# Silu as one ScalarE function instead of tanh and a multiply, in a two-layer sequence kernel

## The chip, the cores and the metric

The kernel runs on one core of a Trainium2 chip. The core has a matmul engine (TensorE, PE in the profile; its weight loads are shown apart as PEld), VectorE (DVE), ScalarE (ACT, the engine of the activation functions), GpSimd (POOL) and SyncE (SP, which here only issues DMAs). The engines run side by side, each through its own list of instructions in order, and wait for one another through semaphores. TensorE writes to PSUM, a small memory of banks; the other operands lie in SBUF. The metric is the device time of one execution in microseconds.

## The reference: what is computed

Two layers work on x of 2 x 1024 tokens with 512 features, each as an attention-like part and a feed-forward part; after every part the result is added to x and normalized over the features. Cut to what matters here:

```python
# layer 0, attention part: silu on q, k and v
q = silu(x @ Wq); k = silu(x @ Wk); v = silu(x @ Wv)      # 16 heads of 32
o = lightning_attn(q, k, v, log_decay)                     # chunks of 128 tokens
o = rmsnorm_per_head(o * sigmoid((x @ Wg1) @ Wg2)) * w
x = layernorm(x + o @ Wo)
# layer 0, feed-forward: silu on the gate, then a Walsh-Hadamard transform
x = layernorm(x + fwht(silu(x @ W1.T) * (x @ W3.T)) @ W2.T)
# layer 1, selective scan: for each of 512 features and 32 states
delta = softplus(dt + b_dt)
h = exp(delta * A) * h + delta * u * B                     # step by step in time
y = sum_over_states(h * C) + u * D
x = layernorm(x + y)
# layer 1, feed-forward: silu on the gate
x = layernorm(x + (silu(x @ Wg) * (x @ Wu)) @ Wdown)
```

All of it is float32.

## The kernel before

**Tiling and phases.** The tokens are cut into five groups (`GROUPS`, line 38): three of four chunks of 128 tokens and two of two chunks, at the beginning and the end of one sequence. A group passes through four phases, listed in `PHASES` (line 40): V computes the values, A is the rest of the attention, F the feed-forward part of layer 0, f that of layer 1. The scan of a group (class `Scan`) runs beside these phases: it begins after the group's F and must be finished before its f. The Hadamard transform is folded into W2 once at the start, on VectorE (`butterflies`) and TensorE (`w2_products`).

**The order of the work.** A planner (`Order`, line 61) builds the program. Every part of the kernel is a generator (a thread) that yields `Op`s: an engine, an estimated duration, the buffers read and written, and a priority. The planner keeps a clock for every engine, finds for each engine the op that can start, takes among ops that are ready the one of the lowest `prio`, and writes the instructions in the order of its own estimated times. So an estimate that is changed reorders the whole program. Estimates of ScalarE's work come from `act` (line 254): 0.26 us and 0.82 ns per column.

**Tables.** ScalarE holds the tables of one set of functions at a time; a function of another set is preceded by an instruction that loads its tables (ACT_TABLE_LOAD in the profile). The planner keeps one name for what is loaded (`self.table`): an op with another `table` gets 1.3 us more, and among ready ops of equal priority one that needs no load goes first (`wrong`, line 161). Before the change there are two names, "tanh" and "log". The set that has tanh has exp too, and so does the set of the logarithm (`natural_log_exp_and_others`, which `log_tables`, line 448, loads). So the exponentials of the scan carry no name: they run with either.

**Silu before.** The product x @ W lies in a PSUM bank. `silu2` (line 531, for q, k and v) has ScalarE write tanh(x/2) to a buffer `th` (through `tanh_half`, line 455), and VectorE then forms (tanh(x/2) + 1) * x, which is twice silu (line 536). In the feed-forward phases `hidden` (line 1014) does the same into the tile h (lines 455 and 1025), and VectorE multiplies by the second product (line 1030). The surplus factors of two are taken out elsewhere: the decays of the attention are scaled by 0.125, the transformed W2 by 0.5, and the last feed-forward phase scales its sum by 0.5 when it is added (line 1072). The attention's sigmoid gate also uses tanh (line 731).

**The scan.** A unit is one state of two blocks of 128 features over a four-chunk group (or of four blocks over a two-chunk group). For a unit GpSimd forms delta * u * B into `dbu` (line 1332, five buffers); ScalarE writes exp(delta * A) into `da`, a pair of PSUM banks with two buffers (line 1352); VectorE runs the recurrence over `da` and `dbu` (line 1379) and multiplies by C (line 1392); GpSimd sums up the results (lines 1422, 1428 and a DMA that accumulates, issued at line 264). If the sequence goes on in a later group, ScalarE copies the last state (line 1404). The `da` buffer comes free when both have read it. The scan's VectorE ops have a priority below that of the attention and feed-forward ops.

**Around silu on TensorE.** All matmul results other than `da` share four PSUM banks ("mm"). `product` (line 986) makes the gate's and the second product of the feed-forward phase (matmul line 994), `sums_of` (line 1049) the product with W2 or the down matrix (line 1053). In the attention `project` makes q and k (line 615), `values` makes v (line 565); k is transposed (line 682) and scaled (line 689), scores are made (line 793) and scaled (line 811), outputs are collected (lines 837 and 845), gated, normalized (lines 864 to 896) and mixed (line 940).

Of the kernel before, what the change touches and what calls it, by code (L numbers as in the profile page):

```python
# [11 lines left out]
ALU = mybir.AluOpType  # L12
# [4 lines left out]
P = 128  # L17
# [43 lines left out]
class Order:  # L61
# [25 lines left out]
    def begin(self, op):  # L87
# [53 lines left out]
    def run(self):  # L141
        while True:
# [6 lines left out]
            for th in list(self.threads):  # L149
# [30 lines left out]
def two_layers(  # L180
# [73 lines left out]
    def act(cols, fn, **kw):  # L254
        return Op("ACT", 0.26 + cols * 0.82e-3, fn, **kw)

# [104 lines left out]
    dmh_b = [Buf() for _ in range(EB)]  # L361
    ident_b, consts_b, decays_b, scan_b, early_b, mask_b, hadamard_b = (Buf() for _ in range(7))

# [10 lines left out]
    def load_consts():  # L374
# [45 lines left out]
        yield Op("ACT", 2.0, decays, r=[consts_b, early_b], w=[raw])  # L420
# [21 lines left out]

        yield Op("ACT", 0.8, state_decays, r=[raw], w=[scan_b])

    class Tables:
        log = False

    def log_tables():

        if not Tables.log:  # L450
            nc.scalar.preload_act_table_set("natural_log_exp_and_others")
        Tables.log = True

    def tanh_half(dst, src):
        nc.scalar.activation(dst, src, AF.Tanh, scale=0.5)  # L455
        Tables.log = False

# [39 lines left out]
    def normalized(gi, c, stage, store=None):  # L497
# [14 lines left out]
        def scales():  # L512
# [8 lines left out]
            "ACT", 1.6, scales, r=[s],  # L521
            w=[xb] if store is not None else [xb, there[gi, c, stage]], table="log", prio=-2,
        )
# [6 lines left out]

    def silu2(dst, bank):

        th = Buf()
        yield act(512, lambda: tanh_half(th.t, bank.t), r=[bank], a=[("th", th)], table="tanh")
        yield dve(
            512, lambda: nc.vector.scalar_tensor_tensor(  # L536
                dst.t, th.t, 1.0, bank.t, ALU.add, ALU.mult
            ),
            r=[bank, th], a=[("h", dst)], free=[bank, th],
        )  # L540
# [12 lines left out]
    def front(gi):  # L553
# [6 lines left out]
        def values(c):  # L560
            bank = Buf()

            def mm():
                for k in range(EB):
                    nc.tensor.matmul(  # L565
                        bank.t, xT.t[:, k, c * P : (c + 1) * P], w_v[k].t,
                        start=k == 0, stop=k == EB - 1,
                    )

            yield pe(  # L570
                mm_us(EB, 512), mm, r=xT.reads(c, c + 1) + w_v, a=[("mm", bank)],
                free=w_v if c == n - 1 else [],
            )
            spawn(silu2(v2[c], bank))

# [6 lines left out]
    def attention(gi, nxt, prio):  # L582
# [26 lines left out]
        def project(j, vb):  # L609
# [14 lines left out]
            )  # L624
            spawn(silu2((qT, kT)[j][vb], bank))

# [20 lines left out]
        def head_decays():  # L647

            for eb in range(EB):
# [15 lines left out]
                if gi == 0:  # L665
                    yield Op("ACT", 1.5, made, r=[early_b, consts_b], a=[("dm", b)])
                    b.written = None
                    yield dve(512, masked, r=[mask_b], w=[b])
                    yield dma(KB256, lambda: dmh[eb], lambda: b.t, r=[b], w=[dmh_b[eb]],
# [4 lines left out]
        def block(vb):  # L674
# [41 lines left out]
            def gate(bank=Buf()):  # L716
# [12 lines left out]
                def tanh():  # L729
                    yield act(  # L730
                        512, lambda: tanh_half(sg.t, bank.t), r=[bank], a=[("sg", sg)],
                        free=[bank], table="tanh",
                    )
# [144 lines left out]
            def norm():  # L878
# [12 lines left out]

                yield Op("ACT", 1.3, rstd, r=[bank], w=[sg], free=[bank], table="log")

# [78 lines left out]

    def ffn(ph, gi, xT, whole, down_scale, store, after=None):

# [4 lines left out]
        for fh in range(halves):  # L979
# [34 lines left out]
            def hidden(f):  # L1014

                t, pg, pu = hT[f], pss[f, 0], pss[f, 1]
                yield act(
                    512, lambda: tanh_half(t.t, pg.t), r=[pg], a=[("h", t)], table="tanh"
                )
                t.written = None  # L1020
                if fh == halves - 1 and f == 7:
                    reached(ph)

                def gated():
                    nc.vector.scalar_tensor_tensor(t.t, t.t, 1.0, pg.t, ALU.add, ALU.mult)  # L1025
# [103 lines left out]
    def w2_products(dq, f, b):  # L1129

        cols = slice(dq * q_d, (dq + 1) * q_d)
        for c4 in range(4):
# [29 lines left out]
    class Scan:  # L1162
# [74 lines left out]
        def softplus(self, k, bank, u):  # L1237
# [11 lines left out]
            def logs():  # L1249
# [9 lines left out]
            yield Op(  # L1259
                "ACT", 4 * (0.25 + T * 0.82e-3), logs, w=[r], a=[("th", a)], table="log",  # L1260
                prio=late,
# [81 lines left out]
        def decays(self):  # L1343
# [157 lines left out]
    def phase(i):  # L1501
# [8 lines left out]
        elif ph[0] == "F":  # L1510
            spawn(scan_inputs(gi), -0.5)
            yield from ffn(ph, gi, results[gi], False, 1.0, None)
        else:
            xT = Columns(gi)
            for c in range(chunks(gi)):
                yield from turn(xT, gi, c, 3)
            yield from ffn(ph, gi, xT, False, 0.5, row_of(gi))

# [81 lines left out]
```

## Time and profile before

| | |
|---|---|
| median of three runs | 1909.76 us (1906.78 to 1911.31) |
| time of the profiled execution | 1910.39 us |
| its span in the trace | 1908.6 us |
| TensorE busy | 1807.7 us, 95% of the span |
| VectorE busy | 1432.8 us, 75% |
| ScalarE busy | 868.4 us, 45% |
| GpSimd busy | 1069.5 us, 56% |
| table loads on ScalarE | 94, of 1283 ns each |

The profile is of one execution. Its page gives busy time by engine, the span in 40 equal slices (each digit the busy share in tenths; PEclk is the clock granted to TensorE, in tenths of full speed), the chain of work that ended last, and groups of instructions by line. The trace behind it can be asked for waits (who waited for whom, total, times, longest), for stretches of time (busy time of each engine in each) and for single instructions in order of time. The tanh of q, k and v appears as `th<-mm`, that of the feed-forward gate as `h<-mm`, and that of the attention's own gate as `sg<-mm`, all at line 455.

### The profile page before, as it was taken

The numbers are of one execution on the slowest core, as the hardware profiler recorded it, in microseconds if no ns is written. First come the engines' busy times: TensorE is split into PE (matmuls) and PEld (weight loads), VectorE is DVE, ScalarE is ACT, GpSimd is POOL, SyncE is SP. The second block draws the span as 40 slices with busy tenths as digits, with TensorE's granted clock in tenths as the row PEclk, the third lists the DMA queues.
The fourth block names the chain that finished last, engine by engine and source line by source line (L and its number), as shares of the span: only waits on it lengthen the run. The fifth ranks groups of instructions, "written<-read, shape, count | busy, mean of one in ns | idle before, by whom it ended". The sixth has DMA issues, their size and how long they took to land.

```text
span 1908.6 us, 19111 instructions
## 1 busy us (share of the span) xinstructions
PE 1807.7 (95%) x6160; PEld 988.7 (52%) x6160; DVE 1432.8 (75%) x1747; ACT 868.4 (45%) x1605; POOL 1069.5 (56%) x558
## 2 busy tenths in 40 slices
PE   6989988999999799998799999999799999999998
PEld 3666544445755454444554454444586444544575
DVE  6521389992217999999899999999989999998221
ACT  2420565442244553458553457555434635743221
POOL 0000156760024778898568988867778886776000
PEclk8999998999999899998799999999899999999999
DMA  8635335662555366776446867767589684665252
GB/s 246 177 120 168 121 105 130 163 165 60 162 165 206 100 175 165 213 187 178 120 122 166 218 145 204 201 204 225 161 231 253 169 210 152 188 177 149 72 160 72
DMA packets 212084, 315.22 MB, mean 165 GB/s; under 512 B 19984, under 2 KB 121744, under 8 KB 211984
## 3 DMA queue, kind: packets, MB, share of 16 engines
q1 hardware_dynamic: 193408, 250.56, 41.9%
q0 software_dynamic: 16272, 59.25, 16.8%
q10 hardware_dynamic: 2304, 4.20, 0.6%
q8 instruction: 49, 0.80, 0.2%
q14 instruction: 51, 0.42, 0.1%
HBM read 236.34 MB, written 18.35 MB: 133 GB/s over the span
## 4 chain that ended last, share of the span: by engine, by line
PE 79%; DVE 12%; ACT 3%; DMA 3%; issue 2%; SPq 1%; POOL 0%; DVEq 0%; ACTq 0%
PE mm L994 43%; PE mm L1053 22%; DVE da L1379 5%; PE mm L615 4%; DVE dbu L1392 2%; PE mm L565 2%; PE mm L940 2%; DVE sc L811 1%; PE mm L793 1%; PE mm L479 1%; SPq L264 1%; PE mm L845 1%; DMA C<-rows 1%; PE mm L837 1%; PE mm L745 1%
## 5 line engine op out<-in xcount | busy, mean ns | idle before, releaser
L994 PE MATMUL mm<-xT,w 128*128 128x256 f32 (+1 forms) x2704 | 898.9, 493 | 9.0 <-DVE h L1025 6.4
L994 PEld LDWEIGHTS mm<-xT,w 128*128 128x128 f32 x2704 | 516.8, 192 | 386.3 <-issue 323.2
L1332 POOL TENSOR_TENSOR dbu<-du,B 128x1024 f32<-128x1024 f32 x256 | 630.7, 2479 | 128.4 <-DMA y<-dbu 111.4
L1352 ACT ACTIVATE da<-delta,a_s 128x512 f32<-128x512 f32 (+1 forms) x640 | 386.4, 605 | 260.9 <-DVE dbu L1392 238.9
L1053 PE MATMUL mm<-w,h 128*128 128x512 f32 x1024 | 449.0, 594 | 2.1 <-DVE xn L1076 2.1
L1379 DVE TENSOR_TENSOR_SCAN da<-da,hlast,dbu 128x512 f32<-128x512 f32 (+1 forms) x384 | 425.4, 1108 | 10.6 <-ACT da L1352 5.3
L1428 POOL TENSOR_TENSOR y<-y,dbu 128x1024 f32<-128x1024 f32 x123 | 306.2, 2490 | 98.9 <-DVE dbu L1392 96.9
L1392 DVE TENSOR_TENSOR dbu<-da,C 128x1024 f32<-128x1024 f32 x256 | 312.3, 1220 | 6.0 <-ACT hlast L1404 0.7
L1053 PEld LDWEIGHTS mm<-w,h 128*128 128x128 f32 x1024 | 194.0, 191 | 234.7 <-issue 226.2
L1379 DVE TENSOR_TENSOR_SCAN da<-da,dbu 128x256 f32<-128x256 f32 (+1 forms) x256 | 245.6, 959 | 6.1 <-ACT da L1352 2.5
L1234 POOL TENSOR_TENSOR xn<-xn,dp 128x512 f32<-128x512 f32 x16 | 23.1, 1452 | 312.6 <-PE mm L479 312.6
L1025 DVE SCALAR_TENSOR_TENSOR h<-h,mm 128x512 f32<-128x512 f32 x128 | 87.1, 680 | 129.0 <-ACT h L455 128.8
L455 ACT ACTIVATE h<-mm 128x512 f32<-128x512 f32 x128 | 76.1, 595 | 220.6 <-PE mm L994 220.0
L1030 DVE TENSOR_TENSOR h<-h,mm 128x512 f32<-128x512 f32 x128 | 87.2, 682 | 84.0 <-PE mm L994 83.4
L1404 ACT COPY hlast<-da 128x2 f32<-128x2 f32 (+1 forms) x160 | 25.4, 159 | 228.1 <-DVE dbu L1392 182.4
L615 PE MATMUL mm<-xT,w 128*128 128x512 f32 (+1 forms) x320 | 118.0, 518 | 3.3 <-DVE sc L811 1.8
L264 POOL DMA_DIRECT2D y<-dbu x113 | 102.5, 907 | 20.3 <-DVE dbu L1392 16.5
L615 PEld LDWEIGHTS mm<-xT,w 128*128 128x128 f32 x320 | 60.2, 193 | 53.5 <-issue 44.1
L514 ACT ACTIVATE rstd<-mv,eps 128x1 f32<-128x1 f32 x64 | 18.6, 290 | 135.9 <-DVE mv L509 135.8
L940 PE MATMUL mm<-w,xT 128*128 128x512 f32 x128 | 66.8, 669 | 12.7 <-DVE xT L896 11.0
L536 DVE SCALAR_TENSOR_TENSOR h<-th,mm 128x512 f32<-128x512 f32 x48 | 32.5, 682 | 45.2 <-ACT th L455 45.0
L565 PE MATMUL mm<-w,xT 128*128 128x512 f32 x128 | 60.7, 623 | 3.1 <-DMA w<-in_wv_dram 2.8
(91 smaller groups left out, 1246.3 us busy)
## 6 DMA issues: line engine op xcount, KB each, us to landing
y<-dbu POOLq DMA_DIRECT2D x113, 512.0 KB, 6.2
w<-in_wgut_dram SPq DMA_DIRECT2D x160, 256.0 KB, 4.1
B<-rows SPq DMA_DIRECT2D x128, 256.0 KB, 4.2
C<-rows SPq DMA_DIRECT2D x128, 256.0 KB, 3.7
w<-in_w1t_dram SPq DMA_DIRECT2D x80, 256.0 KB, 4.4
w<-in_w3t_dram SPq DMA_DIRECT2D x80, 256.0 KB, 4.3
w<-w2h SPq DMA_DIRECT2D x80, 256.0 KB, 4.1
w<-in_wdnt_dram SPq DMA_DIRECT2D x80, 256.0 KB, 2.9
```

Of the source, the lines that this page charges most:

```text
L264: return Op(eng, us, lambda: of.dma_start(dst(), src(), **more), dma=nbytes, **kw)
L565: nc.tensor.matmul(bank.t, xT.t[:, k, c * P : (c + 1) * P], w_v[k].t, start=k == 0, stop=k == EB - 1,)
L615: nc.tensor.matmul(bank.t[:, s * T : (s + 1) * T], w_qk[j][k].t[:, eb * P : (eb + 1) * P], xT.t[:, k, :], start=k == 0, stop=k == EB - 1,)
L940: nc.tensor.matmul(accs[c].t, oT.t[:, k_, c * P : (c + 1) * P], w_o[k_].t, start=k_ == 0, stop=k_ == EB - 1,)
L994: nc.tensor.matmul(bank.t[:, s * T + c0 * P : s * T + c1 * P], blocks[fb // 2][j][k // 2].t[:, k % 2 * 2 * P + k0 : k % 2 * 2 * P + k0 + P ...
L1030: 512, lambda: nc.vector.tensor_mul(t.t, t.t, pu.t), r=[pu], w=[t], free=[pu]
L1053: nc.tensor.matmul(accs[c].t, hT[f // S].t[:, s * T + c * P : s * T + (c + 1) * P], w_d[f].t, start=f == 0, stop=f == 8 * S - 1,)
L1332: 1024, lambda: nc.gpsimd.tensor_mul(self.wide(self.db[i]), self.wide(du), self.row(self.bs, i)),
L1352: nc.scalar.activation(d[:, j, :], self.wide(delta)[:, j, :], AF.Exp, scale=a_s[:, k0 + j, n : n + 1],)
L1379: nc.vector.tensor_tensor_scan(d()[:, j, :], d()[:, j, :], self.wide(db)[:, j, :], init, ALU.mult, ALU.add,)
L1392: 1024, lambda: nc.vector.tensor_mul(self.wide(db), d(), self.row(self.cs, i)),
L1428: 1024, lambda: nc.gpsimd.tensor_add(y.t, y.t, db[i].t), r=o, w=[y],
```

## The change

Silu becomes one ScalarE instruction, from PSUM straight to the tile where it is needed. The VectorE steps at lines 536 and 1025 go, and with them the buffer `th` for q, k and v, and the scalings that took out the factors of two. The attention's sigmoid gate keeps its tanh. The function silu lies in a set of tables that has tanh but not exp. So every op now names the sets that it can run with, the exponentials of the scan too; the planner counts a switch when the loaded set is none of them, and then takes the first one named as loaded. The estimate of a ScalarE op also changes.

```diff
+EXP, LOG, TANH, SILU = ("exp", "log"), ("log",), ("exp", "silu"), ("silu",)
...
+    def switches(self, op):
+        return op.table is not None and self.table not in op.table
...
-        if op.table is not None and op.table != self.table:
+        if self.switches(op):
             us += 1.3
-            self.table = op.table
+            self.table = op.table[0]
...
-                wrong = op.table is not None and op.table != self.table
+                wrong = self.switches(op)
...
     def act(cols, fn, **kw):
-        return Op("ACT", 0.26 + cols * 0.82e-3, fn, **kw)
+        return Op("ACT", 0.18 + cols * 0.81e-3, fn, **kw)
...
-        yield dve(
-            P, lambda: nc.vector.tensor_scalar_mul(early[:, 2, :], early[:, 2, :], 0.125),
-            r=[early_b], w=[mask_b],
-        )
...
-        yield dve(512, lambda: nc.vector.tensor_scalar_mul(q_dec, q_dec, 0.125), r=[raw],
-                  w=[decays_b])
...
     def log_tables():
-        if not Tables.log:
+        if order.table != "log":
             nc.scalar.preload_act_table_set("natural_log_exp_and_others")
-        Tables.log = True
-
-    def tanh_half(dst, src):
-        nc.scalar.activation(dst, src, AF.Tanh, scale=0.5)
-        Tables.log = False
+
+    def silu(dst, src):
+        nc.scalar.activation(dst, src, AF.Silu)
...
-    def silu2(dst, bank):
-        th = Buf()
-        yield act(512, lambda: tanh_half(th.t, bank.t), r=[bank], a=[("th", th)], table="tanh")
-        yield dve(
-            512, lambda: nc.vector.scalar_tensor_tensor(
-                dst.t, th.t, 1.0, bank.t, ALU.add, ALU.mult
-            ),
-            r=[bank, th], a=[("h", dst)], free=[bank, th],
+    def to_silu(dst, bank):
+        yield act(
+            512, lambda: silu(dst.t, bank.t), r=[bank], a=[("h", dst)], free=[bank], table=SILU
         )
...
                 yield act(
-                    512, lambda: tanh_half(t.t, pg.t), r=[pg], a=[("h", t)], table="tanh"
+                    512, lambda: silu(t.t, pg.t), r=[pg], a=[("h", t)], free=[pg], table=SILU
                 )
...
-                def gated():
-                    nc.vector.scalar_tensor_tensor(t.t, t.t, 1.0, pg.t, ALU.add, ALU.mult)
-
-                yield dve(512, gated, r=[pg], w=[t], free=[pg])
-                t.written = None
...
-                    if down_scale != 1.0:
-                        nc.vector.scalar_tensor_tensor(
-                            xb.t, bank.t, down_scale, xb.t, ALU.mult, ALU.add
-                        )
-                    else:
-                        nc.vector.tensor_add(xb.t, bank.t, xb.t)
+                    nc.vector.tensor_add(xb.t, bank.t, xb.t)
...
-                    b.t[:, s4, :].rearrange("p c d -> p (c d)"), bank.t, 0.5 / math.sqrt(FF)
+                    b.t[:, s4, :].rearrange("p c d -> p (c d)"), bank.t, 1.0 / math.sqrt(FF)
...
                         self.T, exp, r=[delta, scan_b] + ([da] if j else []),
                         a=[] if j else [("da", da)],
                         free=[delta] if i + len(self.delta) >= U and j == self.W - 1 else [],
+                        table=EXP,
```

The softplus, the normalizations and the attention's rsqrt carry `table=LOG` in place of `"log"`, the attention gate's tanh `table=TANH`, and the decays that are made once at the start `table=EXP`.

More of the change, by code (lines that the diff above doesn't have):

```diff
@@ L361, in two_layers @@
     dmh_b = [Buf() for _ in range(EB)]
-    ident_b, consts_b, decays_b, scan_b, early_b, mask_b, hadamard_b = (Buf() for _ in range(7))
+    ident_b, consts_b, decays_b, scan_b, early_b, hadamard_b = (Buf() for _ in range(6))
     def load_first():
@@ L412, in decays @@
                 )
-        yield dve(
-            P, lambda: nc.vector.tensor_scalar_mul(early[:, 2, :], early[:, 2, :], 0.125),
-            r=[early_b], w=[mask_b],
-        )
         raw = Buf()
-        yield Op("ACT", 2.0, decays, r=[consts_b, early_b], w=[raw])
-        yield dve(512, lambda: nc.vector.tensor_scalar_mul(q_dec, q_dec, 0.125), r=[raw],
-                  w=[decays_b])
+        yield Op("ACT", 2.0, decays, r=[consts_b, early_b], w=[decays_b], table=EXP)
         yield dma(
@@ L441, in state_decays @@
             nc.scalar.mul(a_s, a_s, -1.0)
-        yield Op("ACT", 0.8, state_decays, r=[raw], w=[scan_b])
-    class Tables:
-        log = False
+        yield Op("ACT", 0.8, state_decays, r=[raw], w=[scan_b], table=EXP)
     def log_tables():
-        if not Tables.log:
+        if order.table != "log":
             nc.scalar.preload_act_table_set("natural_log_exp_and_others")
-        Tables.log = True
-    def tanh_half(dst, src):
-        nc.scalar.activation(dst, src, AF.Tanh, scale=0.5)
-        Tables.log = False
+    def silu(dst, src):
+        nc.scalar.activation(dst, src, AF.Silu)
     class Columns:
@@ L521, in normalized @@
             "ACT", 1.6, scales, r=[s],
-            w=[xb] if store is not None else [xb, there[gi, c, stage]], table="log", prio=-2,
+            w=[xb] if store is not None else [xb, there[gi, c, stage]], table=LOG, prio=-2,
         )
@@ L573, in values @@
             )
-            spawn(silu2(v2[c], bank))
+            spawn(to_silu(v2[c], bank))
         for c in range(n):
@@ L624, in project @@
             )
-            spawn(silu2((qT, kT)[j][vb], bank))
+            spawn(to_silu((qT, kT)[j][vb], bank))
         def gates():
@@ L665, in head_decays @@
                 if gi == 0:
-                    yield Op("ACT", 1.5, made, r=[early_b, consts_b], a=[("dm", b)])
+                    yield Op("ACT", 1.5, made, r=[early_b, consts_b], a=[("dm", b)],
+                             table=EXP)
                     b.written = None
-                    yield dve(512, masked, r=[mask_b], w=[b])
+                    yield dve(512, masked, r=[early_b], w=[b])
                     yield dma(KB256, lambda: dmh[eb], lambda: b.t, r=[b], w=[dmh_b[eb]],
@@ L730, in tanh @@
                     yield act(
-                        512, lambda: tanh_half(sg.t, bank.t), r=[bank], a=[("sg", sg)],
-                        free=[bank], table="tanh",
+                        512, lambda: nc.scalar.activation(sg.t, bank.t, AF.Tanh, scale=0.5),
+                        r=[bank], a=[("sg", sg)], free=[bank], table=TANH,
                     )
@@ L890, in rstd @@
                     nc.scalar.activation(sg.t, sg.t, AF.Exp, scale=-0.5)
-                yield Op("ACT", 1.3, rstd, r=[bank], w=[sg], free=[bank], table="log")
+                yield Op("ACT", 1.3, rstd, r=[bank], w=[sg], free=[bank], table=LOG)
                 def scaled():
@@ L970, in attention, with ffn @@
             yield from turn(nxt, gi, c, 1)
-    def ffn(ph, gi, xT, whole, down_scale, store, after=None):
+    def ffn(ph, gi, xT, whole, store, after=None):
         n, T = chunks(gi), tokens(gi)
@@ L1259, in softplus @@
             yield Op(
-                "ACT", 4 * (0.25 + T * 0.82e-3), logs, w=[r], a=[("th", a)], table="log",
+                "ACT", 4 * (0.25 + T * 0.82e-3), logs, w=[r], a=[("th", a)], table=LOG,
                 prio=late,
@@ L1511, in phase @@
             spawn(scan_inputs(gi), -0.5)
-            yield from ffn(ph, gi, results[gi], False, 1.0, None)
+            yield from ffn(ph, gi, results[gi], False, None)
         else:
@@ L1516, in phase @@
                 yield from turn(xT, gi, c, 3)
-            yield from ffn(ph, gi, xT, False, 0.5, row_of(gi))
+            yield from ffn(ph, gi, xT, False, row_of(gi))
     def scan_inputs(gi):
```

## The prediction

> **What bounds the kernel now.** I read the page's busy shares and slices first, then the chain, then the waits of TensorE, then the groups of ScalarE and VectorE, and last the stages and single stretches of time.
>
> ```profile
> PE 1807.7 (95%) x6160; PEld 988.7 (52%) x6160; DVE 1432.8 (75%) x1747; ACT 868.4 (45%) x1605; POOL 1069.5 (56%) x558
> ...
> PE   6989988999999799998799999999799999999998
> ...
> DVE  6521389992217999999899999999989999998221
> ACT  2420565442244553458553457555434635743221
> ...
> PEclk8999998999999899998799999999899999999999
> ...
> PE 79%; DVE 12%; ACT 3%; DMA 3%; issue 2%; SPq 1%; POOL 0%; DVEq 0%; ACTq 0%
> ```
>
> TensorE is the bound: 95% busy and 79% of the chain. VectorE is as full (9 in nearly every slice from 14 to 36) but falls off some 150 us before the end. TensorE's dips, and the lower granted clock that goes with them, lie in slices 6, 7, 14, 19, 20 and 29: the attention stages. By stage (start:end, then busy us of PE, PEld, DVE, ACT, POOL, then clock):
>
> ```profile
> 215.00:317.00 102.00, 88.11 (x489) 49.93 (x487) 78.97 (x125) 64.72 (x130) 53.34 (x28) 0.92 0.39 117
> ...
> 568.00:683.00 115.00, 103.53 (x538) 56.94 (x537) 92.74 (x124) 64.14 (x112) 69.58 (x35) 0.93 0.51 154
> 683.00:822.00 139.00, 139.00 (x346) 65.33 (x345) 129.38 (x129) 57.37 (x110) 115.10 (x60) 1.00 0.74 193
> 822.00:973.00 151.00, 130.05 (x574) 71.78 (x572) 138.02 (x175) 101.83 (x186) 107.57 (x59) 0.85 0.52 144
> ...
> 1300.00:1385.00 85.00, 71.54 (x348) 43.07 (x347) 81.46 (x106) 43.59 (x76) 63.68 (x34) 0.93 0.71 198
> ```
>
> In the four attention stretches TensorE idles 13.9, 11.5, 21.0 and 13.5 us, 59.8 together; in the feed-forward stretch 683 to 822 not at all, and there a faster VectorE alone buys nothing. Who ends TensorE's waits:
>
> ```profile
> PE mm L682 <- DVE h L536: 7.1, 1, 7.1
> ...
> PE mm L994 <- DVE h L1025: 6.4, 2, 4.0
> PE mm L793 <- DVE h L536: 5.6, 3, 4.2
> ```
>
> Over the whole list VectorE ends 57.8 us of TensorE's waits, ScalarE 24.9, DMAs 9.6. The three rows shown, and 0.5 us more of L536, are all that wait for an instruction that the change removes: 19.6 us.
>
> **The change part by part.** The groups (count | busy us, mean ns | idle before):
>
> ```profile
> L1352 ACT ACTIVATE da<-delta,a_s 128x512 f32<-128x512 f32 x384 | 264.3, 691 | 185.4 <-DVE dbu L1392 170.0 <-DMA delta<-dd 6.3 <-DVE da L1379 3.1
> ...
> L455 ACT ACTIVATE h<-mm 128x512 f32<-128x512 f32 x128 | 76.1, 595 | 220.6 <-PE mm L994 220.0
> L451 ACT ACT_TABLE_LOAD x47 | 60.3, 1283 | 0.8
> L455 ACT ACT_TABLE_LOAD x46 | 59.0, 1283 | 1.6 <-ACT xn L517 0.8
> ...
> L1025 DVE SCALAR_TENSOR_TENSOR h<-h,mm 128x512 f32<-128x512 f32 x128 | 87.1, 680 | 129.0 <-ACT h L455 128.8
> ...
> L536 DVE SCALAR_TENSOR_TENSOR h<-th,mm 128x512 f32<-128x512 f32 x48 | 32.5, 682 | 45.2 <-ACT th L455 45.0
> ```
>
> Removed from VectorE: 128 x 0.680 + 48 x 0.682 = 119.6 us, and two small scalings at the start (0.2 and 0.4 us); the add at L1072 changes its form only (684 ns against 688 at L1076). On ScalarE silu takes tanh's place, 176 times; the nearest row for its own time is the tanh from PSUM, 595 ns, so nothing there.
>
> Added: table loads. Today the scan's exponentials run on tanh's tables and on the logarithm's alike:
>
> ```profile
> 893.72 1.31 ACT L1352 ACTIVATE da<-delta,a_s 128x512 f32<-128x512 f32 x2
> 894.95 0.58 ACT L455 ACTIVATE th<-mm 128x512 f32<-128x512 f32 x1
> 895.43 0.69 ACT L1352 ACTIVATE da<-delta,a_s 128x512 f32<-128x512 f32 x1
> ```
>
> No load stands between these. With silu in a set without exp, each such neighbour costs one. I stepped through ScalarE's instructions in today's order with the diff's sets: 114 switches from silu to exp, 97 back, 42 from log to silu, 26 from silu to log, 21 from exp to log, 4 from log to tanh and the first load, 305 in place of 94. 127 of the 176 tanh stand alone between other table users. So 211 more loads x 1.283 = 271 us on ScalarE: 868 to about 1139 us, 60% of the span. The planner prefers work of the loaded set among ready work, which may save some; the bounds are 94 (all grouped) and 305, and I take 305, because ScalarE idles often enough that mostly one operation is ready.
>
> The Trainium skill, "ScalarE: Activation LUTs", section What ACT_TABLE_LOAD costs, puts 1.28 us of load plus 1.38 us of drain on each switch. This trace has the 1283 ns, and no drain: the load at 884.41 ends at 885.69 and the next ACTIVATE starts at 885.71. By the page's 2.66 us the 40 loads added in the attention stretches would cost 55 us more than by the row, and the forecast would be nearer 1944. The same page's rules for kernel authors (do all of one table set before switching) speak against this change, and the three lines above show the interleaving that it warns of.
>
> *Feed-forward stages.* One silu comes per 6.87 us of TensorE (two products of 3.43). A block of load, silu, load is 1.283 + 0.595 + 1.283 = 3.16 us. What covers it: there are two buffers of decays. At 1218.05 VectorE frees one, ScalarE's copy and two exponentials fill it from 1218.08 to 1219.69, the first half at 1218.97, and it is wanted at 1222.35, after a 0.6 us add that is not always there: 2.8 us of slack. A silu block at the worst place overruns by 0.4 us. Some 108 silus lie beside a scan: 43 us lost against 108 x 0.68 = 73 us given back on VectorE. GpSimd follows close behind (115 of 139 us in 683 to 822), so the scan gains little. TensorE is covered anyway: PSUM banks are released after the silu instead of after the VectorE step, and with four banks a gate's bank is needed again only three products, 10.3 us, later. When the third scan ends (1598.1), TensorE still has eight blocks of the earlier phase's sums to interleave, 8 x 3.43 = 27 us; that is the cover of a later scan. Price here: 0, less half of the 6.4 us of L994 waiting for h, since its other multiply stays: -3.2.
>
> *Attention stages.* The stepping adds 6, 13, 10 and 11 loads in the four stretches, 40 x 1.283 = 51.3 us on a ScalarE that is busy 274 of 453 us (0.6). A load delays something where ScalarE is not idle (0.6), and about half of what is behind it is the scan's, not TensorE's: 51.3 x 0.6 x 0.5 = +15.4. The step from tanh to VectorE leaves TensorE's path: -5.6 - 0.5 = -6.1. Bounds: nothing added and the 6.1 gone; or all 34 silus there paying two loads less one VectorE step, 34 x (2.57 - 0.68) = +64. Behind every silu in ScalarE's order stand the scan's exponentials and the copies that free their buffers, and VectorE's scans wait for those.
>
> *Start.* The 7.1 us at L682 is a multiply behind butterflies on VectorE. Without it the next matmul, L1136, still waits for a DMA until 36.2 us, 2.5 us after that wait's end. I take 0; the bound is -7.1.
>
> *The planner.* ScalarE's cost for 512 columns falls from 0.680 to 0.595 us. That fits reads of PSUM (595) and is 0.10 short for the 384 exponentials (691; 477 against 0.387 for 256 columns), so planned orders will run ahead of ScalarE. No DMA is added or dropped on SP's, GpSimd's or ScalarE's queues (of those on ScalarE's, the output rows, nothing waits but the end, where no scan is left and the loads stay 7), but everything is reordered; I have no row for that, and put +-8 us on it.
>
> *Sum.* 15.4 - 6.1 - 3.2 + 0 = +6.1 us of waits. Idle brings a lower clock: 0.08 x 102 + 0.07 x 115 + 0.15 x 151 + 0.07 x 85 = 45 us of clock lost beside 59.8 us of idle, partly inside it; I add half per us: +9. The profiled execution took 1910.4 us (span 1908.6 plus 1.8 around it), 0.6 above the median of the three runs. So 1919 us.
>
> **The rivals.** *B, VectorE's relief reaches TensorE (faster).* VectorE ends most of TensorE's waits. If the loads fall into ScalarE's 40% idle, the direct waits go (19.6 less the start's 7.1) and a fifth of VectorE's other 38.2 us: -20, 1890. Against it: VectorE's scans refill what is freed, and ScalarE was the cause behind a longest wait of L536, 4.2 us at 894.4: its tanh started at 893.02 behind two exponentials and a load.
>
> *C, the scan becomes the bound.* If plan and chip drift, a silu sits in front of the exponentials waiting for its matmul; ScalarE already idles 220 us before L455 for that. It decides from an overrun of (73 + 27) / 108 = 0.93 us per silu. At 1.4 us: 151 - 73 - 27 = +51, 1961. For it: the underpriced exponentials. Against: VectorE waits only 7.8 us for exponentials today.
>
> *D, the terms cancel:* 1910.
>
> **How the numbers follow.** Forecast (1915 to 1935) 0.40, B 0.34, C 0.18, D 0.08. About 0.2% is what a measurement here can tell from no change: faster 0.34, same 0.08, slower 0.58. The range takes B less its lowest part and C up to 1.4 us per silu: 1884 to 1965.
>
> **What would show it.** Right: 250 to 305 table loads, ScalarE at 1070 to 1140 us, VectorE near 1313; L536 and L1025 gone; TensorE without idle in feed-forward stretches, and idle above 60 us in the attention stages, now ended by h on ScalarE. Wrong: far fewer loads; VectorE waiting over 50 us for exponentials and TensorE idle after 1600 us (C); or attention idle below 50 us (B).

## The result, and the profile after

The changed kernel takes 1921.24 us (median of six runs, 1915.70 to 1923.77) against 1909.74 us of the kernel before (six runs): ratio 1.0058, 95% interval 1.0041 to 1.0075. It is slower by about 11 us. The forecast was 1919 us. The profiled execution took 1921.38 us, with a span of 1919.6 us.

In this part "loads" are table loads, and line numbers are those of the kernel after: silu is line 452, the scan's exponentials 1332, its recurrence 1360, the gate's matmul 986, the product with W2 or the down matrix 1039, the multiply of gate and second product 1016, the transposes of k 674, and the transposes of the scan's output 1438.

The page of the kernel after: busy time and, further down, two rows of the 40 slices, the granted clock, and the chain that ended last by engine.

```profile
PE 1804.4 (94%) x6160; PEld 984.1 (51%) x6160; DVE 1329.0 (69%) x1569; ACT 1122.3 (58%) x1801; POOL 1070.5 (56%) x558
...
PE   6999979999999699998799999899799989999998
...
ACT  2621667752157576779675778676576868761121
...
PEclk8999989999999799999799999999799999999999
...
PE 69%; DVE 14%; ACT 10%; issue 3%; DMA 2%; SPq 1%; POOL 1%; DVEq 0%; POOLq 0%; ACTq 0%
```

VectorE is relieved by 104 us of busy time and ScalarE loaded with 254 us more. TensorE is still the bound, and its busy time is 3.3 us shorter. What grew is its idle time, span less busy: 1908.6 - 1807.7 = 100.9 us before, 1919.6 - 1804.4 = 115.2 us after, 14.3 us more. ScalarE's share of the chain went from 3% to 10%.

The groups of ScalarE, each shape by itself (count | busy us, mean ns | idle before):

```profile
L1332 ACT ACTIVATE da<-delta,a_s 128x512 f32<-128x512 f32 x384 | 261.9, 689 | 88.4 <-DVE dbu L1373 68.6 <-DVE da L1360 10.0 <-DMA delta<-dd 3.7
L452 ACT ACT_TABLE_LOAD x128 | 164.2, 1283 | 5.4 <-PE mm L986 2.4 <-ACT xn L513 0.8
L1332 ACT ACT_TABLE_LOAD x107 | 137.3, 1283 | 1.9
...
L452 ACT ACTIVATE h<-mm 128x512 f32<-128x512 f32 x176 | 104.9, 597 | 254.0 <-PE mm L986 208.2 <-PE mm L606 27.5 <-PE mm L556 16.9
L449 ACT ACT_TABLE_LOAD x47 | 60.3, 1283 | 0.8
```

With eight loads of smaller groups that makes 290, where there were 94. Silu itself costs what tanh did (597 ns against 595).

The stretches shown in the prediction, and two more (973 to 1300 and 1505 to 1762) that hold feed-forward phases beside scans:

```profile
215.00:317.00 102.00, 88.16 (x498) 52.85 (x499) 77.84 (x123) 71.77 (x137) 57.43 (x30) 0.92 0.41 123
...
568.00:683.00 115.00, 97.38 (x501) 53.53 (x500) 89.55 (x108) 68.95 (x111) 67.56 (x34) 0.90 0.47 138
683.00:822.00 139.00, 138.05 (x358) 66.16 (x356) 130.78 (x122) 101.52 (x153) 123.82 (x64) 1.00 0.76 197
822.00:973.00 151.00, 131.00 (x607) 71.11 (x606) 133.42 (x170) 114.98 (x199) 113.95 (x60) 0.93 0.54 149
973.00:1300.00 327.00, 318.10 (x798) 148.33 (x797) 301.62 (x285) 238.40 (x359) 279.52 (x144) 0.98 0.71 189
1300.00:1385.00 85.00, 74.58 (x344) 44.05 (x342) 76.25 (x96) 53.00 (x79) 65.10 (x35) 0.92 0.74 204
...
1505.00:1762.00 257.00, 247.00 (x624) 115.55 (x623) 207.05 (x267) 170.64 (x274) 165.08 (x85) 0.99 0.59 160
```

The two kernels are not at the same piece of work at the same microsecond, so single rows compare roughly. In the four attention stretches TensorE idles 13.8, 17.6, 20.0 and 10.4 us, 61.9 together; before it was 59.8. In the two long feed-forward stretches (973 to 1300 and 1505 to 1762) it idles 8.9 and 10.0 us; in the kernel before the same stretches give 4.7 and 0.4. So most of the new idle time lies in the feed-forward phases, not in the attention. Who ended TensorE's waits, and one row of VectorE's:

```profile
PE mm L674 <- DVE sc L803: 9.5, 4, 4.8
PE mm L1117 <- DMA early<-in_consts_dram: 8.1, 1, 8.1
PE mm L1438 <- DVE xn L1057: 6.5, 1, 6.5
...
PE mm L1438 <- DVE h L1016: 4.0, 1, 4.0
...
PE mm L1039 <- ACT h L452: 2.9, 2, 2.7
...
PE mm L1438 <- ACT h L452: 1.8, 1, 1.8
...
PE mm L674 <- ACT h L452: 1.6, 2, 0.9
```

```profile
DVE da L1360 <- ACT da L1332: 49.4, 46, 3.5
```

The three rows with `ACT h L452` are the only ones in which TensorE waits for silu, 6.3 us in all. VectorE waits 49.4 us for the scan's exponentials, 7.8 before.

Since TensorE does the same matmuls in both kernels, one can also ask when it had done each fortieth of them, counted by the columns that they write. The kernel after is 2.7 to 5.9 us ahead from the second fortieth to the thirteenth (the first gate matmul of the first group starts at 105.05 us instead of 110.59), 5.0 behind at the fourteenth (attention at 614 to 680 us), 6.8 ahead again at the twenty-fifth, and loses the rest between the twenty-fifth and the thirty-third, most of it at 1199 to 1254 and 1544 to 1598 us; it ends 11.0 behind.

### The profile page after: what moved, and what is told of

The parts are those of the page before. It is cut to its first block, busy times and chain, and to the rows that moved or that the text cites. A ratio compares the mean times of both kernels' runs of the same rounds, so it can differ in the third digit from the quotient of the medians.

```text
span 1919.6 us, 19210 instructions
## 1 busy us (share of the span) xinstructions
PE 1804.4 (94%) x6160; PEld 984.1 (51%) x6160; DVE 1329.0 (69%) x1569; ACT 1122.3 (58%) x1801; POOL 1070.5 (56%) x558
## 4 chain that ended last, share of the span: by engine, by line
PE 69%; DVE 14%; ACT 10%; issue 3%; DMA 2%; SPq 1%; POOL 1%; DVEq 0%; POOLq 0%; ACTq 0%
PE mm L986 40%; PE mm L1039 17%; DVE da L1360 8%; PE mm L606 3%; ACT da L1332 3%; DVE dbu L1373 2%; ACT L1332 2%; PE mm L556 2%; ACT L452 1%; PE mm L932 1%; PE mm L785 1%; DVE xT L888 1%; DVE sc L803 1%; ACT h L452 1%; SPq L272 1%
## 5 line engine op out<-in xcount | busy, mean ns | idle before, releaser
L1312 POOL TENSOR_TENSOR dbu<-du,B 128x1024 f32<-128x1024 f32 x256 | 645.8, 2535 | 104.4 <-DMA y<-dbu 85.6
L1409 POOL TENSOR_TENSOR y<-y,dbu 128x1024 f32<-128x1024 f32 x123 | 316.7, 2574 | 88.8 <-DVE dbu L1373 85.0
L452 ACT ACTIVATE h<-mm 128x512 f32<-128x512 f32 x176 | 104.9, 597 | 254.0 <-PE mm L986 208.2
L1057 DVE TENSOR_TENSOR xn<-mm,xn 128x512 f32<-128x512 f32 x56 | 38.3, 684 | 141.4 <-PE mm L1039 141.4
L272 POOL DMA_DIRECT2D y<-dbu x113 | 106.9, 946 | 26.6 <-DVE dbu L1373 22.0
L932 PE MATMUL mm<-w,xT 128*128 128x512 f32 x128 | 64.5, 650 | 12.1 <-DVE xT L888 9.7
```

Source lines behind the costliest of these rows:

```text
L272: return Op(eng, us, lambda: of.dma_start(dst(), src(), **more), dma=nbytes, **kw)
L452: nc.scalar.activation(dst, src, AF.Silu)
L932: nc.tensor.matmul(accs[c].t, oT.t[:, k_, c * P : (c + 1) * P], w_o[k_].t, start=k_ == 0, stop=k_ == EB - 1,)
L1312: 1024, lambda: nc.gpsimd.tensor_mul(self.wide(self.db[i]), self.wide(du), self.row(self.bs, i)),
L1409: 1024, lambda: nc.gpsimd.tensor_add(y.t, y.t, db[i].t), r=o, w=[y],
```

## The experiments

The question was which part of the change carries the 11 us: the loads, the new order of the work, or the silu that now stands between matmul and VectorE; and, within the loads, whether they act in the attention (the prediction's term) or beside the scan in the feed-forward phases (which the prediction priced at 0). "Ratio" is always to the kernel before on the same chip, with five rounds, and 95% intervals. Kernels that are not described against the kernel before are edits of the kernel after.

**The loads taken away, all or by half.** The planner goes on planning for silu, so the order stays that of the kernel after, but the instruction that is sent is tanh, whose tables hold exp too.

```diff
     def silu(dst, src):
-        nc.scalar.activation(dst, src, AF.Silu)
+        nc.scalar.activation(dst, src, AF.Tanh)
```

> The changed kernel's own order of instructions on every engine, with tanh computed where it computes silu: one ScalarE instruction as before, no VectorE step, but a function that shares a set with exp, so 94 table loads in place of 290. It leaves out the multiplication by x, so what it computes is not silu. Theory 1 (the added loads cost the time, the relief of VectorE is worth something): at least 15 us below the changed kernel's 1921, so 1890 to 1905, below the kernel before too. Rival (the loads lie in ScalarE's idle time and the new order of the program costs the time): 1916 to 1924.

Only in the feed-forward phases (so that the loads of the attention are left):

```diff
-                    512, lambda: silu(t.t, pg.t), r=[pg], a=[("h", t)], free=[pg], table=SILU
+                    512, lambda: nc.scalar.activation(t.t, pg.t, AF.Tanh), r=[pg], a=[("h", t)], free=[pg], table=SILU
```

> The changed kernel's order, with true silu for q, k and v and tanh in its place in the feed-forward phases (the multiplication by the gate is left out there): 134 loads. By the prediction's step (loads cost in the attention stretches, nothing in the feed-forward ones): nearly all of the changed kernel's loss is back, 1914 to 1921. Rival (loads cost beside the scan, wherever they are): within 6 us of the run without added loads.

Only for q, k and v (so that the loads of the feed-forward phases are left):

```diff
-            512, lambda: silu(dst.t, bank.t), r=[bank], a=[("h", dst)], free=[bank], table=SILU
+            512, lambda: nc.scalar.activation(dst.t, bank.t, AF.Tanh), r=[bank], a=[("h", dst)], free=[bank], table=SILU
```

> The other half: the changed kernel's order, with true silu in the feed-forward phases and tanh in its place for q, k and v (the multiplication is left out there): 250 loads. By the prediction's step: within 4 us of the run without added loads. Rival (loads beside the scan delay the exponentials, and TensorE behind them): within 6 us of the changed kernel's 1921.

| | loads | median us | ratio (95%) |
|---|---|---|---|
| none of the added loads | 94 | 1907.12 | 0.9983 (0.9974 to 0.9993) |
| those of the attention | 134 | 1907.13 | 0.9986 (0.9975 to 0.9996) |
| those of the feed-forward phases | 250 | 1917.15 | 1.0032 (1.0013 to 1.0051) |
| all (the kernel after) | 290 | 1921.24 | 1.0058 (1.0041 to 1.0075) |

The 196 loads cost 0.0075 of the time, 14.3 us, or 0.07 us each, and without them the change would be a gain of 0.17%. The 40 loads of the attention alone cost nothing that shows (0.0003); the 156 of the feed-forward phases cost 0.0049, 9.4 us. That all together cost 0.0026 more than the feed-forward's alone is within the intervals. The kernel with the feed-forward phases' loads does not take the same time in every execution: nine of its twelve took 1915.62 to 1921.20 us, three 1905.77 to 1907.37, as without added loads. The profiled one is among the nine, so what the three did otherwise is not known.

Where the 14.3 us arise can be read off too, because TensorE's instructions have the same order in the first kernel of the table and in the last. Instruction by instruction the kernel after falls behind by 2.1 us at 37 to 66, 2.9 at 636 to 644, 4.1 at 1101 to 1116, 3.2 at 1234 to 1255, 2.0 at 1347 to 1352 and 3.0 at 1534 to 1546, beside smaller amounts back and forth. Three of these places are in feed-forward phases beside a scan, 10.3 us together. Over whole stretches it loses 2.2 us before 110 us, 7.7 from 973 to 1300 and 3.8 from 1505 to 1762; in the four attention stretches together it gains 0.2, so what single places there lose is made up for.

One of the places, in the kernel after (ScalarE, then TensorE, then VectorE; start, duration, instruction, and in brackets the idle time before it with what ended it):

```profile
1530.16 1.28 ACT L1332 ACT_TABLE_LOAD   x1
1531.46 1.30 ACT L1332 ACTIVATE da<-delta,a_s 128x512 f32<-128x512 f32 x2
...
1538.68 1.28 ACT L452 ACT_TABLE_LOAD   x1
1539.97 0.60 ACT L452 ACTIVATE h<-mm 128x512 f32<-128x512 f32 x1
1540.59 1.28 ACT L1332 ACT_TABLE_LOAD   x1
...
1540.62 4.56 PE L1039 MATMUL mm<-w,h 128*128 128x512 f32 x10 [2.74 <-ACT h L452]
...
1532.25 2.62 DVE L1360 TENSOR_TENSOR_SCAN da<-da,hlast,dbu 128x512 f32<-128x512 f32 x2 [1.39 <-ACT da L1332]
...
1542.68 2.62 DVE L1360 TENSOR_TENSOR_SCAN da<-da,hlast,dbu 128x512 f32<-128x512 f32 x2 [1.37 <-ACT da L1332]
```

The same silu and the exponentials behind it in the kernel without added loads, where tanh is sent for silu:

```profile
1525.30 1.28 ACT L452 ACT_TABLE_LOAD   x1
1526.59 0.60 ACT L452 ACTIVATE h<-mm 128x512 f32<-128x512 f32 x1
1527.09 1.30 ACT L1332 ACTIVATE da<-delta,a_s 128x512 f32<-128x512 f32 x2
```

It looks as if TensorE's 2.74 us were the price of the load in front of silu. But that load stands in both kernels, because a softplus came before it, and without the added loads TensorE starts the same matmul at 1527.30 us with no wait before it. What differs is how late the work on ScalarE and VectorE is: this silu comes 13.4 us later than in the other kernel, while TensorE's matmuls just before are 10.4 us later. TensorE makes up the difference by waiting. What the kernel after adds up to here are loads in front of exponentials, at 1530.16 and at 1540.59, and after each of them VectorE's scan waits, 1.39 and 1.37 us; in the other kernel it has neither wait.

The place in the attention shows how a late scan reaches TensorE:

```profile
635.57 1.28 ACT L1332 ACT_TABLE_LOAD   x1
636.87 2.75 ACT L1332 ACTIVATE da<-delta,a_s 128x512 f32<-128x512 f32 x4
...
638.38 2.50 DVE L1360 TENSOR_TENSOR_SCAN da<-da,dbu 128x512 f32<-128x512 f32 x2 [3.52 <-ACT da L1332]
640.79 1.27 DVE L803 TENSOR_TENSOR sc<-mm,dm 128x512 f32<-128x512 f32 x2
...
641.52 0.90 PE L674 MATMUL mm<-cst,h 128*128 128x128 f32 x3 [4.76 <-DVE sc L803]
```

The load makes the exponentials late, VectorE's two scans wait 3.52 us for them (2.10 without the added loads), and the scaling of the scores, which TensorE's bank hangs on, stands behind the scans in VectorE's fixed order. TensorE waits 4.76 us (2.00 without), and the row of waits names VectorE, not a load. Over all rows of TensorE's waits, the kernel after has 56.0 us ended by VectorE, 32.4 by ScalarE and 16.8 by DMAs; without the added loads these are 42.3, 30.7 and 15.9. So by these rows, of one execution each, most of what the loads cost reaches TensorE through VectorE.

**Only the loads, in the order of before.** In the kernel before, silu's function is sent in tanh's place, and the VectorE step stays:

```diff
-    def tanh_half(dst, src):
-        nc.scalar.activation(dst, src, AF.Tanh, scale=0.5)
+    def tanh_half(dst, src, fn=AF.Silu):
+        nc.scalar.activation(dst, src, fn, scale=0.5)
...
-                        512, lambda: tanh_half(sg.t, bank.t), r=[bank], a=[("sg", sg)],
+                        512, lambda: tanh_half(sg.t, bank.t, AF.Tanh), r=[bank], a=[("sg", sg)],
```

> The order of the kernel before on every engine, VectorE's steps kept, with silu of x/2 computed where it computes tanh of x/2 (so what comes out is not silu): 306 loads in place of 94, in an order that was not planned for them. Theory 1: 212 loads with no relief, 1930 to 1950. Rival (loads hidden): 1908 to 1914.

1971.39 us, ratio 1.0323 (1.0310 to 1.0337), with 306 loads. Here 212 loads that the planner knew nothing of cost 61.7 us, 0.29 us each: four times what they cost in the order that was planned with them and without the VectorE step.

**Only the VectorE step, left out of the feed-forward phases of before.**

```diff
                 def gated():
-                    nc.vector.scalar_tensor_tensor(t.t, t.t, 1.0, pg.t, ALU.add, ALU.mult)
+                    pass
```

> The order of the kernel before, with the VectorE step that makes silu from tanh left out in the feed-forward phases (128 steps, 87 us of VectorE; what comes out there is tanh times the second product, not silu). No loads are added. If a relief of VectorE reaches TensorE (the prediction's rival B): 1885 to 1900. If it stays under the cover that the prediction names (TensorE full in the feed-forward stretches): 1902 to 1909, about the 3.2 us that were put on the banks freed earlier.

1905.27 us, ratio 0.9980 (0.9965 to 0.9995). VectorE has 128 instructions, 87 us, less, TensorE's 6.4 us of waits for that step are gone, and the kernel gains 3.8 us (interval 1.0 to 6.7). That is what this removal gives in this order.

**Only the planner's estimate for ScalarE.** The kernel after with the old one, and the kernel before with the new one:

```diff
     def act(cols, fn, **kw):
-        return Op("ACT", 0.18 + cols * 0.81e-3, fn, **kw)
+        return Op("ACT", 0.26 + cols * 0.82e-3, fn, **kw)
```

> The changed kernel with the planner's old estimate of ScalarE's work (0.26 us and 0.82 ns per column); the program is planned anew. The prediction put +-8 us on reordering without a row. If the new estimate is part of the loss (it is 0.1 us short for each exponential): 1905 to 1916. If not: 1916 to 1926, or worse.

> The kernel before with the new estimate of ScalarE's work alone (0.18 us and 0.81 ns per column). If the new estimate is part of the loss: 1913 to 1922. If reordering is only scatter: within 8 us of 1909.7 either way.

With the old estimate the kernel after takes 1943.40 us, ratio 1.0178 (1.0157 to 1.0199), at 290 loads as well; with the new one the kernel before takes 1910.45 us, ratio 0.9996 (0.9980 to 1.0011). So the same edit is worth nothing in the one pair of orders, where no loads are added, and about 22 us in the other, where they are. The old estimate is nearer to the exponentials (0.680 us for 512 columns against 0.691 measured; the new one says 0.595), so a third kernel gave the exponentials alone their measured time:

```diff
-                    yield act(
-                        self.T, exp, r=[delta, scan_b] + ([da] if j else []),
+                    yield Op(
+                        "ACT", 0.28 + self.T * 0.81e-3, exp, r=[delta, scan_b] + ([da] if j else []),
```

> The changed kernel, complete, with an estimate of its own for the scan's exponentials as the trace has them (0.28 us and 0.81 ns per column: 0.695 us for 512, 0.487 for 256) beside the changed estimate for the rest; planned anew, 288 loads. If the short estimate of the exponentials makes the plan run ahead of ScalarE at a cost: 1900 to 1915. If the plan's remaining loss is not of this kind: 1915 to 1930.

1938.15 us, ratio 1.0147 (1.0131 to 1.0164), 288 loads. A truer estimate made the order worse by 17 us. VectorE's wait for the exponentials in this kernel, and then in the one with the old estimate:

```profile
DVE da L1360 <- ACT da L1332: 63.1, 58, 2.7
```

```profile
DVE da L1360 <- ACT da L1332: 77.9, 64, 5.3
```

Among the kernels planned for silu throughout, the wait goes up roughly with the time: 22.4 us (loads off), 34.3 (attention's loads), 35.9 (feed-forward's), 49.4, 63.1 and 77.9 at 1907, 1907, 1917, 1921, 1938 and 1943 us. That suggested late exponentials as the cause. But the kernel with the loads in the order of before, 1971 us, has only this:

```profile
DVE da L1379 <- ACT da L1352: 16.8, 15, 1.8
```

and the waits of TensorE that are long there are of another kind: it waits 14.6 us at the transposes of k for the VectorE step (`L682 <- DVE h L536`), where the kernel before had 7.1. The VectorE steps themselves wait longer for silu from ScalarE: 170.4 us (`L1025 <- ACT h L455`) and 63.1 (`L536 <- ACT th L455`), where the kernel before had 128.8 and 45.0. So late exponentials are not the only way in which loads cost time.

**Silu for q, k and v alone.** The attention takes silu, the feed-forward phases keep tanh and the VectorE step, with the factors of two that belong to it; once with the new estimate and once with the old:

```diff
-                    512, lambda: silu(t.t, pg.t), r=[pg], a=[("h", t)], free=[pg], table=SILU
+                    512, lambda: nc.scalar.activation(t.t, pg.t, AF.Tanh, scale=0.5),
+                    r=[pg], a=[("h", t)], table=TANH,
...
+                yield dve(512, gated, r=[pg], w=[t], free=[pg])
```

> True silu for q, k and v as in the changed kernel, tanh and the VectorE step as before in the feed-forward phases with their factor of two taken out as before; planned anew with the new estimate: 135 loads. By the runs so far (loads of q, k and v cost next to nothing in the changed kernel's order): 1900 to 1910. By the prediction's step (loads in the attention stretches cost 15 us and more): 1915 to 1925.

> As the version with silu for q, k and v alone, but planned with the old estimate of ScalarE's work: complete, 130 loads, about 40 of them more than before and 32 us less on VectorE. It is the candidate to beat both kernels: if it keeps the gain at the start (5 us) and the attention loads stay hidden, 1900 to 1906. If a new plan scatters by more than such a gain, as the versions planned with other estimates did (1938, 1943): anywhere from 1905 to 1935.

1913.00 us, ratio 1.0016 (1.0001 to 1.0031), 135 loads; with the old estimate 1917.62 us, ratio 1.0048 (1.0033 to 1.0063), 130 loads. The half of the change with few loads isn't a gain either, although it removes all 13.2 us that TensorE waited for the VectorE step at q, k and v: other waits take their place.

**The exponentials taken out of VectorE's way.** To see whether the loads act through late exponentials, these were written to a tile that nobody reads, and the scan took its decays from `dbu`, which GpSimd delivers; the second kernel has the added loads off besides.

```diff
-                            d[:, j, :], self.wide(delta)[:, j, :], AF.Exp,
+                            aside[:, : self.T], self.wide(delta)[:, j, :], AF.Exp,
...
-                            d()[:, j, :], d()[:, j, :], self.wide(db)[:, j, :],
+                            d()[:, j, :], self.wide(db)[:, j, :], self.wide(db)[:, j, :],
```

> The changed kernel's order with all its 290 loads, but the scan's exponentials are written to a spare tile that nobody reads, and VectorE's scan takes its decays from dbu instead (so the scan's result is wrong). Now no scan waits for an exponential and no exponential for a scan. If the loads cost their 14 us because exponentials come late and VectorE, in its order, holds up what TensorE waits for: this run and the next one, without loads, agree within 4 us. If silu itself comes late to TensorE: they stay 10 us and more apart.

> The same, with tanh computed where silu is (the multiplication left out as well), so 94 loads. It is the base of the run above: within 4 us of it if late exponentials are the path, 10 us or more below it if late silu is.

2403.23 us (ratio 1.2580, 1.2559 to 1.2600) with the loads and 2399.75 us (1.2561, 1.2541 to 1.2581) without. The two agree, as they should if late exponentials were all; but the edit made another program of it. The scan became slow, and TensorE, busy for 81% of the span, then waits for VectorE above all (297.6 us with the loads and 311.0 without, against 118.4 and 113.1 for ScalarE), so the pair decides nothing. The largest group of the scan on VectorE and the multiply before it on GpSimd, with the loads:

```profile
L1360 DVE TENSOR_TENSOR_SCAN da<-dbu,hlast 128x512 f32<-128x512 f32 x256 | 592.6, 2315 | 3.6 <-POOL dbu L1313 0.3
...
L1313 POOL TENSOR_TENSOR dbu<-du,B 128x1024 f32<-128x1024 f32 x256 | 720.0, 2821 | 41.9 <-DMA y<-dbu 23.6 <-DMA du<-dd 17.2
```

VectorE now waits for ScalarE's exponentials nowhere; the group is slow in itself (last section).

## Why the prediction was right, and where it was wrong

The direction and the time (1919 against 1921.24) were right. Not every term was: the sum holds because errors of its terms cancel, and that is luck.

*The count of loads and ScalarE's time: right.* 290 loads against 305 stepped through, ScalarE 1122.3 us against at most 1139.

*The price of a load on ScalarE: right.* The load at 1538.68 us, 1.28 long, is followed by silu at 1539.97. The Trainium skill, "ScalarE: Activation LUTs", section What ACT_TABLE_LOAD costs, adds a drain of 1.38 us to each; no row shown here has one, and the forecast of 1944 by it would have been too high by 23 us. The same page's rule to do all work of one table set before switching fits the runs, as taking the 196 switches away gave back 14.3 us; no run groups the silus to test it.

*VectorE: right in what goes, 16 us off in what is left.* The durations of its instructions sum to 122 us less. Its busy time fell by 104, to 1329.0 and not 1313, since overlapping instructions count once in busy time.

*Feed-forward stages, "Price here: 0, ... -3.2": the step that failed.* The gain of 3.2 agrees in size with the 3.8 us for the VectorE step alone (the 3.2 us of the change without its loads hold the start and the attention too). The price 0 for the loads does not: the loads of these phases cost 9.4 us. The reckoning was an average one: an overrun of 0.4 us for each silu against 0.68 us given back and 27 us of cover at the end of the scan. In that sense the cover was there: the last scan ends at 1718 us, 37 us earlier than before, and TensorE isn't held up at the end. But on the way the loads put the scans, and with them the silus in ScalarE's order, behind TensorE, and TensorE lost the time at single places where a bank or an h was wanted at once, as at 1540.62. The prediction's "TensorE is covered anyway", argued from the four banks and three products, is what these places refute: the transposes at line 1438 and the sums at line 1039 ask for the bank or the h sooner than the third product does. (The 1598.1 us that the prediction gives as the end of the third scan is when VectorE begins to add up its output; the recurrence of that group ends at 1582.6.)

*Attention stages, "+15.4" and "-6.1": both too large.* The 40 loads there cost nothing measurable by themselves, the idle time went from 59.8 to 61.9 us, and the largest part of it ends with the scaling of the scores on VectorE (`DVE sc L803`, 21.5 us over the whole run, 13.7 before) and not h on ScalarE. The waits for L536 went, and as the runs of silu in the attention alone show (1.0016), others took their place. That 0.3 of a load's time reaches TensorE (0.6 from ScalarE's share of busy time, and half of that by a guess) was far too much.

*The start, 0: right in its mechanism, 5.5 us off in the sum.* The DMA took over as foreseen: the matmul behind it starts at 36.78 us, 36.23 before. But from 60 to 115 us the new order has less idle time (4.4 us against 6.8) and a higher granted clock (1.00 and 0.95 against 0.92 and 0.90 in the two parts, before and from 80 us), and the first feed-forward phase begins 5.5 us earlier.

*The planner, +-8: too small.* Two other estimates for the same work ended 17 and 22 us later. The choice of estimate is a part of the change at least as large as the loads; the prediction looked only at its sign for the exponentials ("planned orders will run ahead of ScalarE"), and no harm of that drift shows: the order planned with the truer estimate was slower.

*The clock, half a microsecond more for each of idle, 3 of the +9: wrong.* TensorE's idle time grew by 14.3 us and its busy time fell by 3.3; the mean granted clock is 0.969 after and 0.965 before. The idle time did it alone; +6.1 of it was forecast. Nor does the clock follow the idle time closely from stretch to stretch: at 822 to 973 us TensorE idles 20.0 us at 0.93 after, and 21.0 at 0.85 before.

*Rivals.* B (VectorE's relief reaches TensorE, 1890) comes to no more than the two runs without added loads show: 3.2 and 3.8 us, 6.7 at the end of the wider interval. C (the scan becomes the bound) did not happen: the scan ended earlier, though VectorE's wait for exponentials, 49.4 us, came just under the 50 named for it. D, that the terms cancel, would have needed the loads to cost about a quarter of what they did.

*What stays open.* How the 14.3 us divide between silu that comes late by its own load and exponentials that come late to VectorE. The places and the rows of TensorE's waits speak for the exponentials, but the rows name what ended a wait and not why it was late. A third buffer of decays, which would tell, wasn't tried: the kernel gives four of its PSUM banks to "mm" and four to the decays. What the three quicker executions with the feed-forward phases' loads did otherwise is open too. No complete kernel was found that beats the one before.

## What to carry to other kernels

A switch of tables has no fixed price in time: 1.28 us on its engine was 0.29 us in an order that didn't know of it, 0.07 us in one planned with it, and nothing that shows in the attention stages; look for the places where another engine wants the result at once, since cover that is reckoned as an average over a stage does not reach them, and compare one order with and without the loads, since the load that stands next to a wait need not be the one that caused it. Relief of an engine that is not the bound was worth little here (87 us off VectorE gave 3.8), so it can pay for little new work in front of the bound. Where a planner orders the work, its estimates are a variable of their own: change them alone, in both kernels, before putting a difference down to the instructions.

## What the runs showed of the hardware

The recurrence on VectorE over 512 columns took 1286 ns on average when its decays came from PSUM, and 2315 ns when both operands came from the SBUF tile `dbu`; GpSimd's multiply, which runs beside it, rose from 2535 to 2821 ns. The same group in the kernel after, for comparison:

```profile
L1360 DVE TENSOR_TENSOR_SCAN da<-da,hlast,dbu 128x512 f32<-128x512 f32 x256 | 329.2, 1286 | 30.3 <-ACT da L1332 24.5 <-ACT hlast L1385 1.8 <-POOL dbu L1312 0.4
```

The fastest instructions of the two groups take the same time (1276 ns with the decays in PSUM, 1274 with both in SBUF), and the slowest 1293 and 6454 ns. So the place of the operand alone does not slow the scan; that the two engines disturb each other in SBUF fits both rises, but no run here took GpSimd's work away to show it.
